# A relational graph network: weights by matmul, fewer paced gathers, another order at each layer's end

## Chip, core and metric

The kernel runs on one core of a Trainium2 chip. The metric is the device time of one execution in microseconds, taken as the median of the runs shown. A trace of one further execution, taken by the hardware profiler, gives the durations.

The engines are named as in the profile. PE multiplies matrices, DVE is the vector engine, ACT copies and scales, POOL issues the gathers, and SP issues most other transfers.

## What is computed

There are 12500 nodes with 128 features and 200000 edges in 8 relations, sorted by their target node. Two layers run one after the other, and then a residual and a normalization of each row.

```python
W = jnp.einsum('rb,bio->rio', comp, basis)
xw = jnp.einsum('ni,rio->nro', x, W)
msgs = xw[src, et]
seg = dst * N_REL + et
summed = jax.ops.segment_sum(msgs, seg, num_segments=N_NODES * N_REL)
cnt = jax.ops.segment_sum(jnp.ones((msgs.shape[0],), x.dtype), seg, num_segments=N_NODES * N_REL)
mean = summed / jnp.maximum(cnt, 1.0)[:, None]
agg = mean.reshape(N_NODES, N_REL, HIDDEN).sum(axis=1)
return agg + x @ root + bias
# for each layer: h = relu(conv(h)) + h ; at the end: layernorm(x + h)
```

## The kernel before

**Tiles.** The edges are cut into 1563 tiles of 128. Eight tiles make an octet; there are 196, numbered 0 to 195, and the last has three tiles. Each tile is one indirect gather of 128 rows of 512 bytes, issued by POOL (L632). Layer 0 gathers rows of the input x. Layer 1 gathers rows of y_d, a table in DRAM that holds h times each of the eight relation weights, for every node.

**Order.** The program writes its instructions into a `Plan`. `Plan.add` takes the cells that an operation reads and writes, and works out the semaphore waits; each engine runs its own instructions in the order in which they were added. Transfers use semaphore lanes in turn, three of them for gathers ("gq"), and an operation on a lane waits for the one before it on that lane.

**Gathers and pacing.** `gather(l, q)` issues octet q of layer l. The loops call it with `o + AHEAD`, five octets ahead of the octet that PE takes, and there are seven buffers of rows. `slower` says after which gathers POOL also clears a small tile named rest (L641): 256 columns for the first 160 gathers of layer 0, 320 columns for the last 48 of each layer. Before each such memset POOL waits for the one before the previous one.

**Relation weights.** w_sb holds the nine weight matrices of each layer (eight relations and the root). `weight(l, r)` makes one of them on DVE: one multiplication and seven fused multiply-adds over the eight bases (L656 and L661). Layer 0's are made before the loop, behind the masks of octets 0 and 1. Layer 1's are in the list `later`, which the loop takes from when the counting of edges (`prep`) has ended.

**Layer 0.** For octet o, DVE makes one-hot masks dm with the mean's weights in them (`onehot`, L940). PE multiplies the gathered rows by them (`means`, L1015) into two PSUM banks s, and ACT copies these to sT (`take_means`). `product` multiplies sT by the eight weights (L1038) and `take_product` copies the result to ys. `place` puts it with a mask pl (L948) at its nodes (L1069), and adds the root's term (L1071). When a block of 128 nodes has all its edges, `close` makes the two steps of `finish`: DVE adds the carried part and the bias (L1087, L1092), and then forms h (L1111). `end` runs the second step and calls `table` for the block: two halves on PE (L1127), each copied to y_row, and stored to y_d. Blocks run from 0 to 97; the last two are stored by halves, one of which DVE copies (L1134). `batch` runs the copies that are due, and `table_now` does one half at once. The order of the last octets is written out by hand after the loop.

**Layer 1.** Its first gather waits for the whole of y_d. `add_rows` multiplies each octet by masks of 256 columns straight into an accumulator of a block (L1169), with the root's term (L1172). `finish` follows, and for every eight blocks `norm`: transposes on PE (L1194), and statistics, scaling and the store of the output (L1203 to L1222). Two calls of `onehot` lead the loop, and masks have two buffers here.

Of the kernel before, what the change touches and what calls it, by code (L numbers as in the profile page):

```python
# [8 lines left out]
F32 = mybir.dt.float32  # L9
# [290 lines left out]
class Plan:  # L300
# [25 lines left out]
    def add(self, eng, emit, reads=(), writes=(), lane=None, n=1):  # L326
# [9 lines left out]
        for c in reads:  # L336
            if c in self.writer:
                need(raw, self.writer[c])
# [83 lines left out]
def ordered_path(  # L422
# [46 lines left out]
    AHEAD = 5  # L469
    H = R // 2  # L470
# [16 lines left out]
    y_d = dram.tile([N * R, D], F32, name="y_d")  # L487

# [40 lines left out]
    b_sb = b_f(arena).rearrange("p (l b d) -> p l b d", l=L, b=NB)  # L529
# [5 lines left out]
    def h_cells(j):  # L535
# [9 lines left out]
        ("p_r", I32), ("p_rf", F32))}  # L545
# [33 lines left out]
    plan = Plan(tc, {"hw": 8, "aq": 4, "gq": 3})  # L579
# [33 lines left out]
    rest = keep([P, PACE, 320], F32, "rest")  # L613
# [3 lines left out]
    def slower(l, i):  # L617
        if l == 0 and i < 160:
            return 256
        return 320 if i >= T - 48 else 0  # L620

    def gather(l, q):
# [6 lines left out]
        def emit():  # L629
            ins = []  # L630
            for i in range(q * Q, min((q + 1) * Q, T)):
                ins.append(nc.gpsimd.indirect_dma_start(  # L632
                    out=t[:, i - q * Q, :], out_offset=None, in_=x if l == 0 else y_d,
                    in_offset=bass.IndirectOffsetOnAxis(ap=ids[:, i:i + 1], axis=0)))
                n = slower(l, i)
                if n:
                    k = slow[0]
                    slow[0] += 1
                    if k >= PACE:
                        nc.gpsimd.wait_ge(paced, k - PACE + 1)  # L640
                    nc.gpsimd.memset(rest[:, k % PACE, :n], 0).then_inc(paced, 1)  # L641
            return ins

# [43 lines left out]
    def start():  # L687
# [24 lines left out]
        load(b_sb[:, 0], basis[0].rearrange("b i o -> i b o"), [], [("b_sb", 0)])  # L712
# [6 lines left out]
        load(b_sb[:, 1], basis[1].rearrange("b i o -> i b o"), [], [("b_sb", 1)])  # L719
# [95 lines left out]
    def where():  # L815
# [192 lines left out]
    def means(o):  # L1008
# [4 lines left out]
        def emit():  # L1013
            for i in range(n):
                last = nc.tensor.matmul(s_b[i // 4][0][:, i % 4, :], t[:, i, :], d[:, i, :], start=True, stop=True)  # L1015
            return last

        pe(emit, [c] + dc, [s_b[h][1] for h in range(-(-n // 4))])
# [137 lines left out]
    def add_rows(q, k, opens, last):  # L1156
# [5 lines left out]
        reads = [c] + dc  # L1162
        if root_in:
            ht, hc = hT[:, k * P:k * P + rows_of(k)], ("h", k)
            reads += [hc, ("w", 1, R)]

        def emit():
            for i in range(n):
# [317 lines left out]
```

## Time and profile before

| what | value |
|---|---|
| median of 3 runs | 4023.44 us (4021.93 to 4025.25) |
| profiled execution, its own time | 4022.45 us |
| its span in the trace | 4020.1 us |
| POOL busy | 3055.4 us (76%), 3390 instructions |
| PE busy / weight loads | 2535.3 us (63%) / 2052.8 us (51%) |
| DVE busy | 1701.9 us (42%) |
| ACT busy | 387.7 us (10%) |
| gathers of layer 0 / layer 1 | 1563 x 953 ns / 1563 x 944 ns |
| first gather of layer 1 starts at | 2037.83 us |

A busy share is a mean over the span and does not say what the end waits for. "Issue" is time in which an engine waited for nothing that the profile shows. In a group of the profile the numbers after the bar are the busy time in us and the mean of one instruction in ns, and then the idle time before them with what ended it. A line of the timeline or of the chain starts with its start and its duration in us. A wait line has its total, its count and its longest. A matmul of 32-bit floats shows as two records in the trace, so an octet of eight tiles shows as x16.

### The profile page before, as it was taken

The page shows a single profiled execution, that of the slowest core. Times are in us where ns is not written, and L with a number is a line of the kernel's source. Part 1 is how long each engine was busy: PE and PEld are TensorE (multiplying, and loading weights), DVE is VectorE, ACT ScalarE, POOL GpSimd, SP SyncE. Part 2 cuts the span into 40 slices and gives each one's busy share as a digit, 9 for nine tenths or more (in the row PEclk, how much of TensorE's full clock was granted, in tenths as well). Part 3 has the DMA queues.
Part 4 walks back from the last instruction along what each step waited for, and adds up shares of the span by engine and source line. Part 5 has one row for each costly group of instructions (what it writes and reads, how often), then busy time and mean ns, then how long its engine had stood idle before and what let it go on. Part 6 is the DMA issues. An engine that isn't in the chain of part 4 may idle for free.

```text
span 4020.1 us, 32388 instructions
## 1 busy us (share of the span) xinstructions
PE 2535.3 (63%) x11205; PEld 2052.8 (51%) x11205; DVE 1701.9 (42%) x4764; ACT 387.7 (10%) x834; POOL 3055.4 (76%) x3390
## 2 busy tenths in 40 slices
PE   5776677776666666667655565566556555555654
PEld 3555565555555555556544444444444444444443
DVE  7667533333333333333234444444444444444443
ACT  1111122221111111112100000000000000000000
POOL 8887777777777777777857777777777777777777
PEclk8988888888888888888877777777777777777777
DMA  3112233332222222223222222222222222222221
GB/s 106 50 48 53 58 105 100 105 96 83 80 89 81 83 85 79 85 75 95 73 74 53 58 58 63 53 63 64 53 64 63 53 63 53 63 63 53 63 59 45
DMA packets 128800, 282.48 MB, mean 70 GB/s; under 512 B 53855, under 2 KB 61291, under 8 KB 128627
## 3 DMA queue, kind: packets, MB, share of 16 engines
q0 software_dynamic: 100032, 205.07, 19.6%
q1 hardware_dynamic: 25546, 73.59, 5.0%
q10 hardware_dynamic: 3049, 1.67, 0.2%
q8 instruction: 90, 1.47, 0.2%
q14 instruction: 83, 0.68, 0.1%
HBM read 222.52 MB, written 57.60 MB: 70 GB/s over the span
## 4 chain that ended last, share of the span: by engine, by line
POOL 73%; issue 23%; PE 2%; DVE 1%; DMA 1%; ACT 0%; POOLq 0%; DVEq 0%; ACTq 0%; SPq 0%
POOL rows L632 71%; POOL rest L641 2%; DVE w_sb L661 1%; PE s L1015 0%; PE y L1038 0%; PE ct L772 0%; DMA rows<-in_x_dram,idx 0%; DVE dm L940 0%; PE ct L773 0%; PE s L1169 0%; PE pt L1127 0%; POOLq L397 0%; DVE arena L766 0%; DMA arena<-in_dst_dram 0%; PE ct L1038 0%
## 5 line engine op out<-in xcount | busy, mean ns | idle before, releaser
L632 POOL DMA_INDIRECT rows<-y_d,idy x1563 | 1476.0, 944 | 495.6 <-issue 469.5
L632 POOL DMA_INDIRECT rows<-in_x_dram,idx x1563 | 1489.0, 953 | 449.5 <-issue 446.0
L940 DVE TENSOR_SCALAR dm<-cols,near,w 128x256 f32<-128x256 f32 x1563 | 724.0, 535 | 1099.5 <-PE s L1169 732.3
L1169 PE MATMUL s<-dm,rows 128*128 128x256 f32 x2086 | 744.1, 527 | 517.9 <-DMA rows<-y_d,idy 498.9
L1169 PEld LDWEIGHTS s<-dm,rows 128*128 128x128 f32 x2086 | 555.7, 277 | 674.0 <-DVE dm L940 272.4
L1015 PE MATMUL s<-dm,rows 128*128 128x128 f32 x3126 | 572.0, 358 | 510.3 <-DMA rows<-in_x_dram,idx 510.2
L1015 PEld LDWEIGHTS s<-dm,rows 128*128 128x128 f32 x3126 | 528.0, 263 | 636.4 <-DMA rows<-in_x_dram,idx 577.6
L940 DVE TENSOR_SCALAR dm<-cols,kr,w 128x128 f32<-128x128 f32 x1563 | 514.6, 400 | 603.5 <-PE s L1015 491.3
L1169 PE MATMUL ct<-dm,rows 128*128 128x256 f32 x1040 | 365.7, 521 | 263.7 <-DMA rows<-y_d,idy 252.2
L1169 PEld LDWEIGHTS ct<-dm,rows 128*128 128x128 f32 x1040 | 273.8, 274 | 340.0 <-DVE dm L940 153.7
L1038 PE MATMUL y<-w_sb,sT 128*128 128x128 f32 x1824 | 276.0, 316 | 31.9 <-ACT sT L599 31.9
L1038 PEld LDWEIGHTS y<-w_sb,sT 128*128 128x128 f32 x1824 | 268.5, 233 | 37.6 <-ACT sT L599 37.6
L599 ACT ACTIVATE sT<-s 128x512 f32<-128x512 f32 x391 | 213.5, 607 | 223.5 <-PE s L1015 223.5
L1087 DVE TENSOR_TENSOR v<-po,carry 128x128 f32<-128x128 f32 x98 | 28.4, 290 | 479.3 <-PE s L1015 322.9
L1127 PE MATMUL pt<-w_sb,arena 128*128 128x512 f32 x388 | 204.4, 608 | 36.7 <-ACT y_row L599 35.0
L599 ACT ACTIVATE y_row<-pt 128x512 f32<-128x512 f32 x194 | 115.8, 597 | 1152.8 <-PE s L1015 1051.6
L1215 ACT ACTIVATE st<-st,eps 128x8 f32<-128x8 f32 (+1 forms) x13 | 4.0, 308 | 1968.8 <-DVE dm L940 1839.4
L1038 PE MATMUL ct<-w_sb,sT 128*128 128x128 f32 (+1 forms) x1312 | 187.3, 304 | 0.0
L1038 PEld LDWEIGHTS ct<-w_sb,sT 128*128 128x128 f32 (+1 forms) x1312 | 184.1, 223 | 0.8 <-issue 0.8
L1069 PE MATMUL po<-pl,ys 128*128 128x256 f32 x392 | 117.9, 383 | 0.0
L1127 PEld LDWEIGHTS pt<-w_sb,arena 128*128 128x128 f32 x388 | 63.5, 190 | 83.0 <-ACT y_row L599 77.3
L948 DVE TENSOR_SCALAR pl<-cols,pos 128x256 f32<-128x256 f32 x196 | 92.6, 472 | 26.8 <-PE s L1015 17.6
(125 smaller groups left out, 1092.8 us busy)
## 6 DMA issues: line engine op xcount, KB each, us to landing
y_d<-y_row SPq DMA_DIRECT2D x96, 512.0 KB, 2.8
rows<-in_x_dram,idx POOLq DMA_INDIRECT x1563, 2.5
rows<-y_d,idy POOLq DMA_INDIRECT x1563, 2.5
x_g<-in_x_dram SPq DMA_DIRECT2D x24, 512.0 KB
out_dram<-x_g SPq DMA_DIRECT2D x12, 512.0 KB, 3.2
arena<-in_L_gnn_basis_dram SPq DMA_DIRECT2D x2, 512.0 KB
arena<-in_dst_dram ACTq DMA_DIRECT2D x2, 448.0 KB, 11.9
arena<-in_edge_type_dram SPq DMA_DIRECT2D x2, 448.0 KB
```

The costliest lines, as they stand in the source:

```text
L599: act(lambda: nc.scalar.activation(out_t, in_t, AF.Copy), reads, writes)
L632: ins.append(nc.gpsimd.indirect_dma_start(out=t[:, i - q * Q, :], out_offset=None, in_=x if l == 0 else y_d, in_offset=bass.IndirectOffset ...
L641: nc.gpsimd.memset(rest[:, k % PACE, :n], 0).then_inc(paced, 1)
L661: vec(lambda b=b: nc.vector.scalar_tensor_tensor(w_sb[:, l, r, :], b_sb[:, l, b, :], comp_sb[:, c0 + b:c0 + b + 1], w_sb[:, l, r, :], op0= ...
L940: emits.append(lambda i=i: nc.vector.tensor_scalar(t[:, i - q * Q, :wide], cols[:, :wide], ids[:, i:i + 1], w[:, i:i + 1], op0=ALU.is_equa ...
L948: emits.append(lambda: nc.vector.tensor_scalar(o[:m], cols[:m], pos[:m, g // (2 * R), g % (2 * R):g % (2 * R) + 1], None, op0=ALU.is_equal))
L1015: last = nc.tensor.matmul(s_b[i // 4][0][:, i % 4, :], t[:, i, :], d[:, i, :], start=True, stop=True)
L1038: last = nc.tensor.matmul(y[:m], t[:, r, :nt, :].rearrange("p t k -> p (t k)"), w_sb[:, 0, r, :], start=(r == 0), stop=(r == R - 1))
L1069: ins = nc.tensor.matmul(a, o[:m], t[:m], start=opens, stop=last and not root_in)
L1087: emits.append(lambda: nc.vector.tensor_add(v[:, :n], a[:, :n], t[:, :n]))
L1127: pe(lambda: nc.tensor.matmul(hb[:n].rearrange("p r d -> p (r d)"), hT[:, j * P:j * P + n], w_sb[:, 1, k * H:(k + 1) * H, :].rearrange("p ...
L1169: ins = nc.tensor.matmul(a, t[:, i, :], d[:, i, :], start=(opens and i == 0), stop=(last and i == n - 1))
```

## The change

It does three things. `weights` makes all eight relation matrices of a layer by two matmuls: the bases are loaded as (basis, group of rows) by (row in group, column), a matrix `mixer` holds the coefficients of both layers spread over those groups, ACT copies the products to a y_row buffer, and two transfers on SP write them to w_d in DRAM and read them back into w_sb in the layout needed. `slower` now paces the first 96 gathers of layer 0 and no others. And the last six octets of each layer are gathered two octets ahead of PE instead of five, behind a wait (`after`) for the octet that PE has last been given; the last but one octet is gathered and multiplied in two halves. The order of the last octets of layer 0 is written out anew, and its loop ends two octets earlier. There are four gather lanes.

```diff
-    def add(self, eng, emit, reads=(), writes=(), lane=None, n=1):
+    def add(self, eng, emit, reads=(), writes=(), lane=None, n=1, after=()):
...
-        for c in reads:
+        for c in (*reads, *after):
...
+    CLOSE = 2
+    LATE = 6
...
+    w_d = dram.tile([L, R * D, D], F32, name="w_d")
...
-    b_sb = b_f(arena).rearrange("p (l b d) -> p l b d", l=L, b=NB)
+    b_sb = b_f(arena).rearrange("p (l c) -> p l c", l=L)
...
+    pick = keep([P, NB + K], F32, "pick")
+    mix = keep([P, L * R], F32, "mix")
+    mixer = keep([P, L * R, K], F32, "mixer")
...
-    plan = Plan(tc, {"hw": 8, "aq": 4, "gq": 3})
+    plan = Plan(tc, {"hw": 8, "aq": 4, "gq": 4})
...
-    rest = keep([P, PACE, 320], F32, "rest")
+    rest = keep([P, PACE, 256], F32, "rest")
...
     def slower(l, i):
-        if l == 0 and i < 160:
-            return 256
-        return 320 if i >= T - 48 else 0
+        return 256 if l == 0 and i < 96 else 0
...
-        plan.add("POOL", emit, reads, [cell], lane="gq", n=min(Q, T - q * Q))
-
-    def weight(l, r):
-        c0 = (l * R + r) * NB
-
-        def emit0():
-            return nc.vector.tensor_scalar(w_sb[:, l, r, :], b_sb[:, l, 0, :], comp_sb[:, c0:c0 + 1], None,
-                                           op0=ALU.mult)
-
-        vec(emit0, [("b_sb", l), "comp"], [("w", l, r)])
-        for b in range(1, NB):
-            vec(lambda b=b: nc.vector.scalar_tensor_tensor(
-                w_sb[:, l, r, :], b_sb[:, l, b, :], comp_sb[:, c0 + b:c0 + b + 1], w_sb[:, l, r, :],
-                op0=ALU.mult, op1=ALU.add), [], [("w", l, r)])
+
+        def some(i0, i1):
+            def emit():
+                ins = []
+                for i in range(i0, i1):
+                    ins.append(nc.gpsimd.indirect_dma_start(
+                        out=t[:, i - q * Q, :], out_offset=None, in_=x if l == 0 else y_d,
+                        in_offset=bass.IndirectOffsetOnAxis(ap=ids[:, i:i + 1], axis=0)))
...
+        i0, n = q * Q, in_quad(q)
+        after = [("done", l)] if q >= NQ - LATE else []
+        if q == NQ - 2:
+            for h in range(2):
+                plan.add("POOL", some(i0 + h * 4, i0 + h * 4 + 4), reads, [cell + (h,)], lane="gq", n=4, after=after)
+        else:
+            plan.add("POOL", some(i0, i0 + n), reads, [cell + (0,), cell + (1,)], lane="gq", n=n, after=after)
+
+    def gathers(l, o):
+
+        if o + AHEAD < NQ - LATE:
+            gather(l, o + AHEAD)
+        elif NQ - LATE <= o + CLOSE < NQ:
+            gather(l, o + CLOSE)
+        return o + CLOSE == NQ - 1
+
+
+    def mixers():
+        for op, val, a, f in ((ALU.logical_shift_right, 4, "p_b", "p_bf"), (ALU.bitwise_and, K - 1, "p_r", "p_rf")):
+            vec(lambda op=op, val=val, a=a: nc.vector.tensor_single_scalar(small[a], part, val, op=op), ["part"], [a])
+            vec(lambda a=a, f=f: nc.vector.tensor_copy(small[f], small[a]), [a], [f])
+        vec(lambda: nc.vector.tensor_scalar(pick[:, :NB], iota_f[:, :NB], small["p_bf"], None, op0=ALU.is_equal),
+            ["iota", "p_bf"], ["pick0"])
+        vec(lambda: nc.vector.tensor_scalar(pick[:, NB:NB + K], iota_f[:, :K], small["p_rf"], None, op0=ALU.is_equal),
+            ["iota", "p_rf"], ["pick1"])
+        c3 = comp_sb.rearrange("p (m b) -> p m b", b=NB)
+        vec(lambda: nc.vector.tensor_tensor(c3, c3, pick[:, None, :NB].to_broadcast([P, L * R, NB]), op=ALU.mult),
+            ["pick0"], ["comp"])
+        vec(lambda: nc.vector.tensor_reduce(mix, c3, axis=AX.X, op=ALU.add), ["comp"], ["mix"])
+        vec(lambda: nc.vector.tensor_tensor(mixer, mix.unsqueeze(2).to_broadcast([P, L * R, K]),
+                                            pick[:, None, NB:NB + K].to_broadcast([P, L * R, K]), op=ALU.mult),
+            ["mix", "pick1"], ["mixer"])
+
+    def weights(l, banks):
+        o, oc = yr_r.tiles[l], ("y_row", l)
+        of = o.rearrange("p r d -> p (r d)")
+        for h in range(2):
+            b, bc = banks[h]
+            pe(lambda b=b, h=h: nc.tensor.matmul(b.rearrange("p t d -> p (t d)"),
+                                                 mixer[:, l * R:(l + 1) * R, :].rearrange("p r k -> p (r k)"),
+                                                 b_sb[:, l, h * 4 * P:(h + 1) * 4 * P], start=True, stop=True),
+               ["mixer", ("b_sb", l)], [bc])
+            copy(of[:, h * 4 * P:(h + 1) * 4 * P], b.rearrange("p t d -> p (t d)"), [bc], [oc + (h,)])
+        load(w_d[l].rearrange("(p i) o -> p (i o)", i=R), of, [oc + (0,), oc + (1,)], [("w_d", l)])
+        load(w_sb[:, l, :R, :], w_d[l].rearrange("(r i) o -> i r o", r=R), [("w_d", l)], [("w", l, r) for r in range(R)])
...
-        load(b_sb[:, 0], basis[0].rearrange("b i o -> i b o"), [], [("b_sb", 0)])
+        load(b_sb[:, 0], basis[0].rearrange("b (h i) o -> (b h) (i o)", i=R), [], [("b_sb", 0)])
...
-        load(b_sb[:, 1], basis[1].rearrange("b i o -> i b o"), [], [("b_sb", 1)])
+        load(b_sb[:, 1], basis[1].rearrange("b (h i) o -> (b h) (i o)", i=R), [], [("b_sb", 1)])
...
-        for op, val, a, f in ((ALU.bitwise_and, G - 1, "p_in", "p_inf"), (ALU.logical_shift_right, 3, "p_g", "p_gf"),
-                              (ALU.bitwise_and, K - 1, "p_r", "p_rf")):
+        for op, val, a, f in ((ALU.bitwise_and, G - 1, "p_in", "p_inf"), (ALU.logical_shift_right, 3, "p_g", "p_gf")):
...
-        pe(emit, [c] + dc, [s_b[h][1] for h in range(-(-n // 4))])
+        def some(i0, i1):
...
+        if o == NQ - 2:
+            for h in range(2):
+                pe(some(4 * h, 4 * h + 4), [c + (h,)] + dc, [s_b[h][1], ("done", 0)])
+        else:
+            pe(some(0, n), [c + (0,), c + (1,)] + dc, [s_b[h][1] for h in range(-(-n // 4))] + [("done", 0)])
...
+        if q == NQ - 2:
+            for h in range(2):
+                pe(some(4 * h, 4 * h + 4), [c + (h,)] + dc + more, [ac, ("done", 1)])
+        else:
+            pe(some(0, n), [c + (0,), c + (1,)] + dc + more, [ac, ("done", 1)])
...
-    for q in range(2):
-        onehot(0, q)
-    for r in range(R):
-        weight(0, r)
+    onehot(0, 0)
+    mixers()
+    weights(0, po_b)
+    onehot(0, 1)
...
-    later = [lambda r=r: weight(1, r) for r in range(R)] + [lambda b=b: check_edges(b) for b in range(B)]
+    later = [lambda: weights(1, (pt_b, pt_b))] + [lambda b=b: check_edges(b) for b in range(B)]
...
-    for o in range(NG - 1):
-        gather(0, o + AHEAD)
+    for o in range(NG - 3):
+        gathers(0, o)
...
-    for i in (g - 2, g - 1):
-        onehot(0, NQ, i)
+    def placed(o):
+        close(place(o))
+        for step in opened:
+            step()
+        opened.clear()
+        end()
+
+    gathers(0, g - 2)
+    for step in opened:
+        step()
+    opened.clear()
     batch(None)
     end()
-    close(place(g - 3))
+    product(g - 3)
+    onehot(0, g, g - 4)
+    placed(g - 5)
+    take_product(g - 3)
+    placed(g - 4)
+    onehot(0, NQ, g - 3)
+    placed(g - 3)
+    while len(tables) > 2:
+        table_now()
+    means(g - 2)
+    take_means(g - 2)
+    onehot(0, NQ, g - 2)
+    product(g - 2)
+    take_product(g - 2)
+    while tables:
+        table_now()
+    placed(g - 2)
+    onehot(0, NQ, g - 1)
     onehot(0, NQ, g)
+    means(g - 1)
+    take_means(g - 1)
+    means(g)
+    take_means(g)
     product(g - 1)
     take_product(g - 1)
-    opened.pop()()
-    end()
-    place(g - 2)
-    while tables:
-        table_now()
-    means(g)
-    take_means(g)
-    close(place(g - 1))
-    opened.pop()()
-    end()
-    table_now()
     product(g)
     take_product(g)
-    table_now()
-    close(place(g))
-    opened.pop()()
-    end()
-    while tables:
-        table_now()
+    placed(g - 1)
+    placed(g)
+    now = tables[:]
+    tables.clear()
+    for h in (0, 2):
+        for a, _ in now[h:h + 2]:
+            a()
+        for _, b in now[h:h + 2]:
+            b()
...
-        gather(1, q + AHEAD)
-        if q + AHEAD == NQ - 1:
+        if gathers(1, q):
             pool(lambda: nc.gpsimd.drain())
```

More of the change, by code (lines that the diff above doesn't have):

```diff
@@ L544, in ordered_path @@
         ("nb_i", I32), ("nb_n", F32), ("p_in", I32), ("p_inf", F32), ("p_g", I32), ("p_gf", F32),
-        ("p_r", I32), ("p_rf", F32))}
+        ("p_r", I32), ("p_rf", F32), ("p_b", I32), ("p_bf", F32))}
+    pick = keep([P, NB + K], F32, "pick")
+    mix = keep([P, L * R], F32, "mix")
+    mixer = keep([P, L * R, K], F32, "mixer")
     sel = keep([P, G, K], F32, "sel")
@@ L627, in gather @@
         ids = idx if l == 0 else idy
[L629 to L642, printed above, removed]
         b = q * Q // P
@@ L649, in gather @@
             reads += [("y_d", j) for j in range(NT - 2)] + [("y_d", j, k) for j in (NT - 2, NT - 1) for k in (0, 1)]
-        plan.add("POOL", emit, reads, [cell], lane="gq", n=min(Q, T - q * Q))
-    def weight(l, r):
-        c0 = (l * R + r) * NB
-        def emit0():
-            return nc.vector.tensor_scalar(w_sb[:, l, r, :], b_sb[:, l, 0, :], comp_sb[:, c0:c0 + 1], None,
-                                           op0=ALU.mult)
-        vec(emit0, [("b_sb", l), "comp"], [("w", l, r)])
-        for b in range(1, NB):
-            vec(lambda b=b: nc.vector.scalar_tensor_tensor(
-                w_sb[:, l, r, :], b_sb[:, l, b, :], comp_sb[:, c0 + b:c0 + b + 1], w_sb[:, l, r, :],
-                op0=ALU.mult, op1=ALU.add), [], [("w", l, r)])
+        def some(i0, i1):
[5 more added lines that the diff above has]
+                        in_offset=bass.IndirectOffsetOnAxis(ap=ids[:, i:i + 1], axis=0)))
+                    n = slower(l, i)
+                    if n:
+                        k = slow[0]
+                        slow[0] += 1
+                        if k >= PACE:
+                            nc.gpsimd.wait_ge(paced, k - PACE + 1)
+                        nc.gpsimd.memset(rest[:, k % PACE, :n], 0).then_inc(paced, 1)
+                return ins
+            return emit
@@ L1011, in means, with emit @@
         n = in_quad(o)
[L1013 to L1016, printed above, removed]
-        pe(emit, [c] + dc, [s_b[h][1] for h in range(-(-n // 4))])
+        def some(i0, i1):
+            def emit():
+                for i in range(i0, i1):
+                    last = nc.tensor.matmul(s_b[i // 4][0][:, i % 4, :], t[:, i, :], d[:, i, :], start=True, stop=True)
+                return last
+            return emit
+        if o == NQ - 2:
[3 more added lines that the diff above has]
+            pe(some(0, n), [c + (0,), c + (1,)] + dc, [s_b[h][1] for h in range(-(-n // 4))] + [("done", 0)])
         plan.mark("PE")
@@ L1161, in add_rows, with some, emit @@
         root_in = opens and k >= 0
-        reads = [c] + dc
+        more = []
         if root_in:
             ht, hc = hT[:, k * P:k * P + rows_of(k)], ("h", k)
-            reads += [hc, ("w", 1, R)]
-        def emit():
-            for i in range(n):
-                ins = nc.tensor.matmul(a, t[:, i, :], d[:, i, :], start=(opens and i == 0),
-                                       stop=(last and i == n - 1))
-                if i == 0 and root_in:
-                    nc.tensor.matmul(a[:, :rows_of(k)], w_sb[:, 1, R, :], ht, start=False, stop=False)
-            return ins
-        pe(emit, reads, [ac])
+            more += [hc, ("w", 1, R)]
+        def some(i0, i1):
+            def emit():
+                for i in range(i0, i1):
+                    ins = nc.tensor.matmul(a, t[:, i, :], d[:, i, :], start=(opens and i == 0),
+                                           stop=(last and i == n - 1))
+                    if i == 0 and root_in:
+                        nc.tensor.matmul(a[:, :rows_of(k)], w_sb[:, 1, R, :], ht, start=False, stop=False)
+                return ins
+            return emit
+        if q == NQ - 2:
[3 more added lines that the diff above has]
+            pe(some(0, n), [c + (0,), c + (1,)] + dc + more, [ac, ("done", 1)])
         plan.mark("PE")
@@ L1352, in ordered_path @@
     g = NG - 1
-    assert parts is None and not later and not turned_to and not opened
+    assert parts is None and not later and not turned_to
     def table_now():
```

## Prediction

> **What bounds the kernel now.** I read the page's chain first, then its groups with shapes kept apart, then the waits, then the chain and timeline around the layer's turn.
>
> ```profile
> POOL 73%; issue 23%; PE 2%; DVE 1%; DMA 1%; ACT 0%; POOLq 0%; DVEq 0%; ACTq 0%; SPq 0%
> ...
> POOL rows L632 <- issue: 915.4, 3120, 0.3
> POOL rows L632 <- DMA y_d<-y_row: 26.1, 1, 26.1
> ...
> L641 POOL MEMSET rest<- 128x256 f32 x160 | 53.4, 334 | 0.1
> ...
> L641 POOL MEMSET rest<- 128x320 f32 x96 | 36.6, 381 | 0.1
> ```
>
> 96% of the chain is POOL and its issue time. Of the 4020 us, 3126 gathers use 1489.0 + 1476.0 us and the 915.4 us of issue time between them. POOL waits for other engines once, 26.1 us for layer 0's table; PE makes it wait 1.1 us in all. So what POOL no longer does is time, and what leaves DVE, PE or ACT is not, unless POOL waits for it.
>
> The next lines (POOL in the timeline) give the pitch with and without pacing.
>
> ```profile
> 1938.88 0.94 POOL L632 DMA_INDIRECT rows<-in_x_dram,idx  x1 [0.30 <-issue]
> 1940.13 0.94 POOL L632 DMA_INDIRECT rows<-in_x_dram,idx  x1 [0.30 <-issue]
> 1941.08 0.38 POOL L641 MEMSET rest<- 128x320 f32 x1
> 1941.62 0.95 POOL L632 DMA_INDIRECT rows<-in_x_dram,idx  x1 [0.17 <-issue]
> 1942.57 0.38 POOL L641 MEMSET rest<- 128x320 f32 x1
> 1943.12 0.95 POOL L632 DMA_INDIRECT rows<-in_x_dram,idx  x1 [0.17 <-issue]
> ```
>
> An unpaced gather comes every 1.248 us, one with a 320 memset every 1.495. In the chain near 106 us, gathers with a 256 memset start at 106.58 and 108.02: 1.442. Each memset thus costs 0.247 or 0.194 us of POOL, less than its own 0.38 or 0.33, since part of it lies in issue time.
>
> The last view is PE in the timeline, late in layer 0 (the last line is from the chain).
>
> ```profile
> 1907.74 2.05 PE L1015 MATMUL s<-dm,rows 128*128 128x128 f32 x16
> 1917.72 3.78 PE L1015 MATMUL s<-dm,rows 128*128 128x128 f32 x16 [3.04 <-DMA rows<-in_x_dram,idx]
> 1927.67 2.05 PE L1015 MATMUL s<-dm,rows 128*128 128x128 f32 x16 [1.69 <-DMA rows<-in_x_dram,idx]
> ...
> 1984.69 3.28 PE L1015 MATMUL s<-dm,rows 128*128 128x128 f32 x16 [2.30 <-DMA rows<-in_x_dram,idx]
> ...
> 2008.53 3.23 PE L1015 MATMUL s<-dm,rows 128*128 128x128 f32 x16 [2.26 <-DMA rows<-in_x_dram,idx]
> ...
> 2034.77 2.29 DMA y_d<-y_row
> ```
>
> Unpaced octets come every 10.0 us, and PE waits for each one's landing, about 1.6 us after its last gather is issued. Even at full rate PE keeps up with POOL. Octet 194 starts on PE at 2008.53, octet 195's last gather is issued by 2011.3 (it lands near 2012.9), and layer 1's first gather starts at 2037.83, behind the y_d store.
>
> **The change, part by part.**
>
> *Start pacing.* Memsets go from gathers 96 to 159: 64 x 0.194 = **12.4 us**, all on POOL. Is there cover for the faster pace? Octets 21 to 34 are already unpaced while the counts of later blocks run, and their gathers start every 10.1 to 10.4 us; PE waited for them. So octets 12 to 19 should run like that.
>
> A rule bears on this. Row first: in the chain one gather at 142.78 took 2.47 us, not 0.95; the long ones of the first 400 us lie mostly over the f16 comparisons of L766, and the stretch above 0.945 adds up to about 12.8 us in layer 0. The Trainium skill (SBUF — State Buffer, Who interferes with whom) says that a VectorE instruction with two SBUF inputs contends with a GpSimd one that reads SBUF. Taken alone, it prices the removed w_sb operations, two SBUF inputs each, at up to their 39.4 us as gain, and lets the unpaced gathers meet more L766. The trace disagrees on the first: gathers during the w_sb stage (29 to 52 us) keep the 11.5 us octet, and w_sb overlaps account for about 0.4 us of stretch. I take 0 for w_sb, and for L766 the same stretch as now, because the number of those operations is unchanged: bounds -3 to +4 us.
>
> *Weights.* Removed: 64 DVE operations per layer, in the first layer from 28.92 to 52.41, 23.5 us; in the second the same beside gathers. Added on DVE: four 128x1 operations (0.15 each by L822/L823), two masks (0.31 by L826), a product and a reduction over 128 columns (0.29 each by L859/L860), a 128x256 product (0.5, by the 0.44 of L828): 2.3 us. Two of the small ones come out of the later placement code. Per layer also two 128x512 matmuls (1.1 each by L1127), two ACT copies (0.6 each), a 512 KB store to DRAM (2.8, by the y_d row) and its read back in 512-byte pieces. No row shows that read; it lies between the 2.3 of y_d and, with other work, 7.8 of the root load; I take 3.5. With dm of octet 0 done at 26.4, layer 0's weights arrive about 26.4 + 2.3 + 2.2 + 0.7 + 2.8 + 3.5 = 38, up to 43, instead of 52.4. They are first needed by product(0), and POOL does not need PE's first octet until gather 56, at 88 us. So this gives POOL **0**; if the cover were gone the bounce would cost 6 to 11 us once. Queues: on SP the two DMAs stand behind x_g (its issue ends near 27.7) and SP waits there for ACT; behind it are only later loads of x. ACT's queue is passed by two copies. In layer 1 the weights go between octets 27 and 42, with SP idle, and the first table is at 42. One instruction order matters: PE's means(0) now stands behind the weight matmuls, at about 31 instead of 27.2; nothing waits for it before 88 us.
>
> *Lead.* The last six gathers of a layer also wait for PE's octet three back. PE ends that octet about 6 us after its landing, some 12 us before POOL wants to issue (octet 187 on PE ends near 1929.7; gather 190 would start near 1946). So **0**. Behind a blocked gather on POOL stand all later gathers and, in layer 1, only the drain. The fourth lane and the half-and-half octet 194 add one wait each: 0.
>
> *End of layer 0.* Gathers 1515 up to octet 192's landing lose 28 memsets, 6.9 us: PE starts 192 at 1984.7 - 6.9 = 1977.8 on this run's clock, before the start's gain. From there I follow PE's new order, with octet 192 at 0 and the landings of 193, 194, 195 at 10, 20 and 23.7. Means 192 (3.5), product 191 (2.4) and a placement: 6.4. Product 192 (1.95), placements 190 to 192 with their DVE steps: 11.1. Four table halves of blocks 93 and 94 at 1.81 (2019.07 to 2020.88 in the chain), PE free at 17.6. Means 193 (2.05) 19.7, its ACT copies 1.1, product 193: 22.8. The halves of 95: 25.6, placement 193: 26.6. Means 194 and 195 (2.05 + 0.83): 29.4. Products 194 and 195 (3.9): 33.3. Placements 194, 195 (1.7): 35.0. Four last halves, copied on ACT and DVE by turns: last copy out at 40.0. Store 2.3, POOL's start 0.75: 43.0. So layer 1 starts at 1977.8 + 43.0 = 2020.8, not 2037.8: **17.0 us**. PE, no longer POOL, sets this stretch: everything has landed by 23.7.
>
> Here the second rule matters. The rows: sixteen matmuls take 2.05 us after continuous work and 3.78 after a 3 us wait. The skill (TensorE: Matmul & The Clock Gate, What's actually happening) says that an idle window drops the array to half clock and that some 3.4 us of work restore it. In the new order PE is rarely idle after octet 192, so I take warm durations. Were it cold throughout, three means add 1.7 and four products 1.1 each, about 8 to 10 us, and the gain is 8. If instead the order were limited by octet 195's landing alone, the last steps (means, products, placements, halves, store) take about 15 us after it, and the gain is 21.6. Range 8 to 21.6.
>
> *End of layer 1.* Octet 193 lands 36 x 0.247 = 8.9 us earlier. Now PE's octet 193 (6.8), dm (1.5), wide (0.3), and the normalization of eight slots on PE and DVE run to about 16.2 after its landing, and the last v follows at 17.1; before it was at 4005.19 - 3986.39 = 18.8. Gain 8.9 + 1.7 = **10.6**. Bounds 9 (half-octet gives nothing) to 12.5 (all 48 memsets and shorter). The final store and exit are unchanged.
>
> Sum: 12.4 + 0 + 17.0 + 10.6 = 40.0 us. The profiled execution took 4022.45 (span 4020.1), so 3982.4; the median of the runs shown is 1.0 higher: **3983 us**.
>
> **The rivals.**
> *Late PE at the turn* (20%). PE runs cold or is already late at octet 192; only 8 of the 17 remain: 3992. For: octets 191 to 192 hold 9.7 us of PE work (1996.62 to 2006.27 shows one like it), close to the 10.0 pitch. Against: two rows in three at that pitch are warm.
> *Ideal turn* (14%): PE has caught up, and less stretch by L766 adds 3: 40 + 4.6 + 3 gives 3975.
> *Pacing protected the gathers* (6%): without memsets the gathers of octets 12 to 19 stretch as much as the memsets took; the start gives 0: 3995. Against: octets 21 to 27.
> *Lead becomes a serial wait* (4%), slower: if PE ends the octet three back later than POOL finishes the two between, over 14 us behind its landing, each of 12 late octets waits for PE. At 4.5 us each this is 54 us, against the 40 gained: 4037. It decides only from 3.4 us per octet. The trace shows PE under 7 us behind.
> That the weights arrive late is no rival with this size: it would need 45 us more.
>
> **How the numbers follow.** The main case has 56%, range 3978 to 3988. With late PE, ideal turn and the stretch beside it, the range is 3972 to 3995; outside lie the ends of these and the lead. 0.2% is 8 us, about what a measurement of this kernel can tell from no change. All but the lead, and 2% of odd sums, are faster by more: 0.94; same 0.02; slower 0.04.
>
> **What would show it.** Memsets: 96 of 128x256, none of 320. Gathers 96 to 159 every 1.25 to 1.29 us; the last 48 of each layer every 1.25. L656 and L661 of w_sb gone, PE's octet 2 near 50 and not 72 us, yet POOL's octets 0 to 11 where they were. POOL's wait on y_d near 21 us, from 26.1. POOL waits on PE below 2 us. It is wrong if POOL waits for s or for a PE semaphore in the late octets, if gathers 96 to 159 keep 1.4 us, or if that wait on y_d grows.

## The result, and the profile after

The changed kernel takes 3979.64 us (median of 5 runs, 3978.35 to 3979.88). Beside it the kernel before took 4023.44 us (5 runs, 4021.93 to 4025.65). The ratio is 0.989, with a 95% interval of 0.9875 to 0.9904. The prediction was 3983 us in a range of 3972 to 3995, so time and direction were right. The profiled execution took 3979.88 us, with a span of 3978.1.

First the page's chain, which answers to the one shown of before:

```profile
POOL 74%; issue 23%; PE 2%; DMA 1%; DVE 0%; POOLq 0%; ACT 0%; ACTq 0%; SPq 0%
```

Then POOL's groups with shapes kept apart:

```profile
L645 POOL DMA_INDIRECT rows<-in_x_dram,idx x1563 | 1488.2, 952 | 465.0 <-issue 460.0 <-DMA arena<-in_dst_dram 2.5 <-PE y L1084 0.6
L645 POOL DMA_INDIRECT rows<-y_d,idy x1563 | 1476.6, 945 | 495.1 <-issue 495.1
L654 POOL MEMSET rest<- 128x256 f32 x96 | 31.9, 332 | 0.1
```

And its longest wait line, with the total, the count and the longest single wait:

```profile
POOL rows L645 <- issue: 955.1, 3117, 19.2
```

POOL still bounds the kernel, with 97% of the chain. The gathers take what they took (952 and 945 ns, before 953 and 944). Of the 256 memsets 96 are left. The issue time is 955.1 instead of 915.4 us. Of the 39.7 more, 20.5 are pauses that a removed memset no longer covers (160 of them, each 0.30 instead of 0.17 us, make 20.8). The other 19.2, the longest, is the wait at the turn of the layers, which this trace puts under "issue" and not under y_d.

The chain at that turn shows what it really is:

```profile
2001.69 0.70 DVE y_row L1180
2002.39 0.02 issue
2002.40 2.54 DMA y_d<-y_row
...
2005.07 1.00 issue
2006.07 0.94 POOL rows L645
```

The last half of the table is copied, stored in 2.54 us, and POOL starts layer 1 at 2006.07, before at 2037.83.

To place the gain I cut the span at three gathers of POOL. The second pair of profiles comes from the experiments, where both kernels ran once more on a chip on which the kernel before takes 4023 us.

| stretch of POOL | before, two profiles | after, two profiles | gain | predicted |
|---|---|---|---|---|
| start to layer 0's octet 188 | 1926.4, 1926.8 | 1913.5, 1914.7 | 12.9, 12.1 | 12.4 |
| octet 188 to layer 1's first gather | 111.4, 112.5 | 92.6, 92.6 | 18.8, 19.9 | 17.0 |
| that gather to layer 1's octet 188 | 1878.2, 1878.3 | 1879.1, 1879.9 | -0.9, -1.6 | 0 |
| octet 188 to the end of the span | 104.1, 105.2 | 92.9, 94.1 | 11.2, 11.1 | 10.6 |
| sum | 4020.1, 4022.8 | 3978.1, 3981.3 | 42.0, 41.5 | 40.0 |

### The profile page after: what moved, and what is told of

Read it like the earlier page. It is cut to its first block, busy times and chain, and to the rows that moved or that the text cites. A ratio compares the mean times of both kernels' runs of the same rounds, so it can differ in the third digit from the quotient of the medians.

```text
span 3978.1 us, 32124 instructions
## 1 busy us (share of the span) xinstructions
PE 2532.4 (64%) x11213; PEld 2046.9 (51%) x11213; DVE 1660.6 (42%) x4643; ACT 390.6 (10%) x838; POOL 2997.6 (75%) x3230
## 4 chain that ended last, share of the span: by engine, by line
POOL 74%; issue 23%; PE 2%; DMA 1%; DVE 0%; POOLq 0%; ACT 0%; ACTq 0%; SPq 0%
POOL rows L645 73%; POOL rest L654 1%; PE s L1055 0%; DMA rows<-in_x_dram,idx 0%; PE y L1084 0%; PE pt L1173 0%; PE ct L1084 0%; POOLq L398 0%; PE s L1216 0%; PE po L1115 0%; DVE x_g L1275 0%; DMA y_d<-y_row 0%; DMA rows<-y_d,idy 0%; DMA idx<-in_src_dram 0%; ACT y_row L606 0%
```

## The experiments

The twelve runs fell on three chips of the same kind. On chip A the kernel before takes 4023 us, on chip B about 4655 and on chip C 4611, so each run is compared with the kernel before on its own chip. The first expectations, those of chip B, were written with chip A's times in mind; the later ones give numbers for both sorts of chip.

### On chip A: the change again, its lead, its table halves

The changed kernel once more:

> The changed kernel itself, on the chip of the experiments. Where PE keeps up with the gathers (the kernel before takes about 4023 us) it should take 3980 us, ratio 0.989. Where PE lags the landings by some 70 us (the kernel before takes about 4653 us) the serial-wait reading says that octet 190's first gather waits 30 to 35 us behind PE in layer 0 and about 10 to 15 us in layer 1, so that it ends near the other kernels with the lead of two, 4716 to 4740 us, above the kernel before. The rival says the loss of those kernels came from their own edits (more pacing, less pacing, DVE weights), and then this one takes at most what the kernel before takes there, about 4610 to 4655 us.

Measured: 3980.23 us (3978.01 to 3983.2), before 4023.43, ratio 0.9891 (0.9875 to 0.9908). The result repeats. The kernel before, for a second profile:

> The kernel before, for a profile on the chip of the experiments. Where PE lags by some 70 us: PE is the bound of both layers' bodies, so octets 20 to 188 are as far behind the gathers as in the kernel with only the pacing changed; the stage from PE's octet 189 to layer 1's first gather takes about 58 to 65 us, against 86 to 90 with the lead of two. If the kernel with only the pacing changed lost its 0.7% by PE's clock, the bodies of the layers and not the stages at their ends will be shorter here.

Measured: 4025.05 us in one execution; its stretches are in the table above. This chip was of the first sort, so the comparison of PE-bound bodies that it was meant for did not come about.

Next, the lead of five for all octets and no wait for the octet last given to PE:

```diff
-        after = [("done", l)] if q >= NQ - LATE else []
+        after = []
...
-        if o + AHEAD < NQ - LATE:
-            gather(l, o + AHEAD)
-        elif NQ - LATE <= o + CLOSE < NQ:
-            gather(l, o + CLOSE)
-        return o + CLOSE == NQ - 1
+        gather(l, o + AHEAD)
+        return o + AHEAD == NQ - 1
```

> The changed kernel with the lead of five throughout and without the wait for the octet that PE has last been given; everything else as changed. Where PE keeps up: the wait has never ended last, so no difference to the changed kernel (within 3 us, about 3980 us). Where PE lags by some 70 us: octet 190's gather no longer waits in either layer, PE's octet 189 to layer 1's first gather takes about 58 us instead of 86 to 90, and PE's octet 189 of layer 1 to its end about 49 instead of 59, so some 40 us less than the changed kernel. If the lead is not what costs there, both take the same within the noise of 25 us, and the two stages are the same.

Measured: 3977.26 us (3975.86 to 3978.12), ratio to before 0.9885 (0.9869 to 0.9902). That is 3.0 us under the changed kernel on the same chip, at the edge of the 3 us that were called no difference. POOL's stretches are 1913.8, 90.7, 1878.4 and 92.6: the late gathers keep their pitch, so the wait costs POOL nothing. Of the 1.9 us at the turn, 1.6 are PE's, in octet 192. PE in the timeline, first of this kernel, then of the changed one:

```profile
1965.02 2.05 PE L1052 MATMUL s<-dm,rows 128*128 128x128 f32 x16 [0.56 <-DMA rows<-in_x_dram,idx]
1966.91 1.95 PE L1081 MATMUL ct<-w_sb,sT 128*128 128x128 f32 x16
```

```profile
1964.74 3.64 PE L1055 MATMUL s<-dm,rows 128*128 128x128 f32 x16 [3.03 <-DMA rows<-in_x_dram,idx]
1968.21 1.95 PE L1084 MATMUL ct<-w_sb,sT 128*128 128x128 f32 x16
```

The same sixteen matmuls take 2.05 us behind a table half with 0.56 us idle, and 3.64 after 3.03 us idle. From their start to the product it is 1.89 against 3.47. The second profile of the changed kernel has this for octets 191 and 192:

```profile
1955.99 3.54 PE L1055 MATMUL s<-dm,rows 128*128 128x128 f32 x16 [1.46 <-DMA rows<-in_x_dram,idx]
...
1965.97 3.67 PE L1055 MATMUL s<-dm,rows 128*128 128x128 f32 x16 [1.54 <-DMA rows<-in_x_dram,idx]
```

So octets were slow after 1.46 and 1.54 us idle, while a line shown of before was warm (2.05) after 1.69; the idle time alone does not say which it will be. The trace does say why a half stood next to octet 192 with the lead of five: octet 191 was slow there (3.78 us), its products were slow too (2.86), and the half behind them ended only 0.56 us before octet 192 landed. But octet 191 was fast (2.00) in one profile of the changed kernel and slow (3.54) in the other, so this changes from execution to execution. The 1.6 us cannot be put down to the lead.

Last, table halves on two PSUM banks for five blocks instead of two:

```diff
         split = j >= NT - 2
+        other = j >= NT - 5
...
-            hb, bc = ct_b if split and k == 1 else pt_b
+            hb, bc = ct_b if other and k == 1 else pt_b
```

> The changed kernel with the two halves of the table alternating between two PSUM banks for the last five blocks of layer 0 instead of the last two. The turn of the layers is bound by PE; where a half on one bank waits for the copy of the half before it, a half is issued after about 1.8 us instead of 1.1. Expected: PE's octet 192 to layer 1's first gather 2 to 4 us shorter than in the changed kernel, and nothing elsewhere: a ratio of 0.999 to the changed kernel, which the times alone hardly show. A rival says that the copies on ACT set the pace whichever bank they come from, and the stage is as long as before.

Measured: 3977.82 us (3977.45 to 3981.07), ratio to before 0.9887 (0.987 to 0.9903), which does not part it from the changed kernel. The stage is 1.6 us shorter (octet 192 on PE to layer 1's first gather 39.7 against 41.3 in both profiles of the changed kernel; octet 192 is slow in all three), just below the expected 2 to 4. PE in the timeline of this kernel says where the rest went:

```profile
1976.74 1.02 PE L1174 MATMUL pt<-w_sb,arena 128*128 128x512 f32 x2
...
1979.41 1.02 PE L1174 MATMUL ct<-w_sb,arena 128*128 128x512 f32 x2
1980.27 1.95 PE L1055 MATMUL s<-dm,rows 128*128 128x128 f32 x16
...
1987.65 1.95 PE L1055 MATMUL s<-dm,rows 128*128 128x128 f32 x16
1991.94 0.91 PE L1055 MATMUL s<-dm,rows 128*128 128x128 f32 x6 [2.34 <-DMA rows<-in_x_dram,idx]
```

The four halves of blocks 93 and 94 take 3.5 us instead of 6.3 (1975.00 to 1981.30 in the changed kernel), and the two of block 95, behind octet 193, take 1.7 instead of 2.7. So the rival, that ACT's copies set the pace, is out. But of these 3.7 us PE gives back most: it now reaches octet 195 before its rows have landed and waits 2.34 us for them, where the changed kernel did not wait. There PE's work and the landing of octet 195 are nearly in balance at the turn, and a shorter PE order alone has little more to give.

### On chips B and C: where PE does not keep up

Five kernels ran on chip B and three on chip C. They were to split the gain by part. That failed, since POOL is not the bound there. The measured times stand together in a table behind the expectations.

More start pacing, 160 gathers, in the changed kernel:

```diff
-        return 256 if l == 0 and i < 96 else 0
+        return 256 if l == 0 and i < 160 else 0
```

> The changed kernel with the memset after each of the first 160 gathers of layer 0 again, instead of 96. Theory (each memset is POOL time and PE keeps up either way): 64 x 0.194 = 12.4 us more by the pitches, up to 13.4 by the start of octet 20 in the two traces; 3992 to 3993 against 3979.6, all of it between octets 12 and 20. Rival (the start gained because the weights left DVE, and the memsets are hidden): 3980 and octet 20 near 231.

Pacing at both layers' ends, in the changed kernel:

```diff
-        return 256 if l == 0 and i < 96 else 0
+        if l == 0 and i < 96:
+            return 256
+        return 320 if i >= T - 48 else 0
```

> The changed kernel with the 320-column memset after each of the last 48 gathers of both layers again. Theory: octet 192 of layer 0 lands 6.9 us later and the PE work behind it follows unchanged, with about 2 more because octet 195 now lands after PE wants it; in layer 1 10.6 to 12 more. Together 19 to 21 us: 3999 to 4001. Rival (the end of layer 0 is bound by PE's order alone, so that late landings are free there): 10.6 to 12 us only, 3990 to 3992. Rival (the memsets spared the matmuls or the landings something): under 3985.

No pacing, in the changed kernel:

```diff
-        return 256 if l == 0 and i < 96 else 0
+        return 0
```

> The changed kernel with no memset at all. Theory: 96 x 0.194 = 18.6 us off POOL; PE's first octet ends near 37 us and octet 7 would be gathered from about 75, so no wait: 3961. Rival (gathers are stretched by the f16 comparisons of the counting as the pace rises, or PE, which takes 8.5 to 9 us an octet there, makes POOL wait): half of it, 3970. Rival (the first memsets protect the input transfers, and without them everything starts later): 3980 or more.

Only the new pacing, in the kernel before (on chip B, then once more on C):

```diff
-        if l == 0 and i < 160:
-            return 256
-        return 320 if i >= T - 48 else 0
+        return 256 if l == 0 and i < 96 else 0
```

> The kernel before with one edit: memsets after the first 96 gathers of layer 0 and nowhere else; DVE weights, lead of five, old order. Theory: start 12.4 to 13.4; layer 0's end only by the landing of octet 194, 10.9, because PE's old order takes 29.3 us from there; layer 1's end 9 to 12. Together 32 to 36 us: 3987 to 3991. The rest, 8 to 11 us, would be the new order's. Rival (pacing is everything): 3980. Rival (the old order falls behind at the faster pitch, PE late): 3996 or more.

> The kernel before with only the pacing of the changed kernel (96 gathers of layer 0), lead, order and weights as before. Where PE keeps up (before about 4023 us): the start gains 12.4 us, the octets at each layer's end come every 10 us instead of 12, so octet 194 of each layer lands about 10.7 us earlier. In before the turn takes 29.3 us from octet 194's means to layer 1's first gather; if that stays, layer 1 starts 23 us earlier and the end gains another 9 to 10.5, in all 33 to 35 us, 3988 to 3991 us, ratio 0.9915 to 0.992. The rest of the changed kernel's gain, 8 to 10 us, is then the new order and the halves. If the order of before makes PE late already from octet 192 on, the turn gains less, the total is 25 to 30 us, 3993 to 3998 us. Where PE lags by some 70 us it takes about 0.7% longer than the kernel before again.

Weights on DVE, in the changed kernel (on B, then on C):

```diff
-    onehot(0, 0)
-    mixers()
-    weights(0, po_b)
-    onehot(0, 1)
+    for q in range(2):
+        onehot(0, q)
+    for r in range(R):
+        weight(0, r)
...
-    later = [lambda: weights(1, (pt_b, pt_b))] + [lambda b=b: check_edges(b) for b in range(B)]
+    later = [lambda r=r: weight(1, r) for r in range(R)] + [lambda b=b: check_edges(b) for b in range(B)]
```

> The changed kernel with the relation weights made on DVE again (64 operations a layer, bases loaded as before, no mixer, no matmuls, no transfers through w_d); pacing, lead and order as changed. Theory (POOL sets the time and does not wait for PE at the start): no difference, within 2 us of the changed kernel, where that takes 3979.6; octet 20 of layer 0 is gathered from 231 to 233 and PE's octet 2 runs near 72 instead of 54. Rival (the start gained because PE is ready earlier): PE's first octets 20 us later make POOL wait in octets 7 to 14, up to 20 us slower. Rival (the weights through DRAM cost time): faster by 2 to 10 us. If PE is the slower engine in this run, the first rival's 20 us should show in full.

> The changed kernel with the weights made by 128 two-operand instructions on DVE as before; pacing, lead and order as changed. Where PE keeps up: the matmul weights are hidden, so no difference to the changed kernel, 3978 to 3982 us, ratio 0.989; octet 0's product waits for the weights until about 55 us and the catch-up on PE is over before octet 20. The rival (reads of weights and bases by DVE stretch the gathers of POOL) expects 5 to 10 us more, lying between octets 2 and 30.

No pacing, lead of five and halves on two banks, three of the edits above together:

```diff
-        return 256 if l == 0 and i < 96 else 0
+        return 0
...
-        after = [("done", l)] if q >= NQ - LATE else []
+        after = []
...
+        gather(l, o + AHEAD)
+        return o + AHEAD == NQ - 1
...
+        other = j >= NT - 5
```

> The changed kernel with three more edits: no pacing at all, the lead of five throughout, and the table halves alternating banks for the last five blocks of layer 0. Where PE keeps up: without the 96 memsets the start gains 96 x 0.194 = 18.6 us more (octet 20 starts at about 213 instead of 232), the turn 1.5 to 3 us, nothing at the end: 3956 to 3960 us, ratio 0.983 to 0.985. The rival that the remaining pacing protects the first gathers from colliding with something (loads of the start, PE not yet through with the buffers) expects that the start gives back half of it or more: octet 20 at 222 or later, 3965 to 3980 us.

| kernel, chip | median us | before there | ratio, 95% |
|---|---|---|---|
| more start pacing, B | 4740.06 (two near 4704, two near 4772) | 4653.04 | 1.0187 (1.0086 to 1.0288) |
| pacing at the ends, B | 4720.91 | 4653.04 | 1.0102 (1.0011 to 1.0194) |
| no pacing, B | 4736.76 | 4653.04 | 1.0163 (1.0089 to 1.0236) |
| only the new pacing, B | 4689.61 | 4653.04 | 1.0069 (1.0031 to 1.0108) |
| weights on DVE, B | 4715.76 | 4657.34 | 1.0147 (1.006 to 1.0234) |
| only the new pacing, C | 4658.1 | 4610.76 | 1.009 (1.0067 to 1.0113) |
| weights on DVE, C | 4657.6 | 4610.76 | 1.0092 (1.0066 to 1.0119) |
| three edits, C | 4681.36 | 4610.76 | 1.0136 (1.0088 to 1.0184) |

All are slower than the kernel before there, though the kernels of chip B lie too close together for their spread of up to 72 us to be ranked. The expectation for only the new pacing on C, written after chip B's result, gave about 0.7% more time for this case; it is 0.9%. The times that the other expectations give are for a PE that keeps up, and none was reached here. The profile of the kernel with only the new pacing, on chip C, shows what the bound is there. Span and mean granted clock of its core:

```profile
core 0: 4653.1 us, clock 0.732
```

The page's busy row and chain:

```profile
PE 2431.6 (52%) x11205; PEld 1924.6 (41%) x11205; DVE 1696.3 (36%) x4764; ACT 387.2 (8%) x834; POOL 3004.7 (65%) x3230
...
another core or an unknown queue 44%; PE 22%; DVE 18%; issue 11%; ACT 4%; DMA 0%; POOL 0%; DVEq 0%; POOLq 0%; ACTq 0%; SPq 0%
```

POOL's waits:

```profile
POOL rows L630 <- remote: 480.0, 137, 9.9
POOL rows L630 <- PE s L1013: 166.2, 27, 9.4
```

POOL's share of the chain is 0%. It waits some 650 us in these two lines together; the second is for buffers that PE has not freed, and that the 480 us of the first ("remote", a release that the profile does not show) are the same is likely but not shown. PE's mean granted clock is 0.73 there, 0.80 to 0.81 on chip A. PE's matmuls do not fill the time either: it is busy 52% of the span and stops for up to tens of microseconds in between. It does not stop alone. Of the kernel with more start pacing, PE, ACT and DVE in the timeline:

```profile
261.29 1.95 PE L1055 MATMUL s<-dm,rows 128*128 128x128 f32 x16
316.12 3.42 PE L1084 MATMUL y<-w_sb,sT 128*128 128x128 f32 x16 [52.87 <-issue]
```

```profile
314.98 1.08 ACT L606 ACTIVATE sT<-s 128x512 f32<-128x512 f32 x2 [54.56 <-remote]
```

```profile
314.98 0.29 DVE L1133 TENSOR_TENSOR v<-po,carry 128x128 f32<-128x128 f32 x1 [56.14 <-remote]
```

PE, ACT and DVE stand for over 50 us and start again within 1.2 us of each other, while POOL issues 42 gathers. The six profiles of the kernels on chip A, with the two of the result, have no stretch of over 8 us in which none of the three works. The eight of chips B and C have 74 to 86 each, 927 to 1234 us in sum. POOL issues gathers in every one of these 627 stops, and in none is there a memset: they lie where the gathers are not paced.

The kernels without any pacing stop from the start. DVE and then POOL in the timeline of no pacing, on chip B:

```profile
54.58 0.72 DVE L806 TENSOR_TENSOR arena<-arena 128x153 f16<-128x153 f16 x4 [21.01 <-issue]
77.01 0.70 DVE L806 TENSOR_TENSOR arena<-arena 128x157 f16<-128x157 f16 x4 [21.71 <-remote]
```

```profile
103.61 0.94 POOL L645 DMA_INDIRECT rows<-in_x_dram,idx  x1 [29.17 <-PE s L1055]
```

From 22 us on the counting of edges stands for 11, 20 and 21 us with little work between. PE begins its first octet at 101.1 us (34.4 in the changed kernel on chip A), and POOL waits 29 us for it at octet 7. Octet 12 is gathered at 163.5 us and not at 148.0 as with more start pacing, from which this kernel differs by its memsets alone; with three edits on chip C it is 161.3, with weights on DVE 148.4. So the memsets that were to cost 18.6 us saved 13 to 16 us there. The rival of the last expectation, that pacing protects the first gathers, said octet 20 at 222 us or later; it is at 264.4 on B and 262.3 on C. Pacing at the ends points the same way, though that kernel as a whole is not faster: octet 180 on PE to layer 1's first gather takes 159.5 us with it, and 172.8 to 178.4 in the other changed kernels of chip B. By what a stream of unpaced gathers stops the other engines, and why not on chip A, no run shows. Nor is it shown whether the lower clock there is a cause or a consequence of a PE that stands so often.

After such a stop PE stays 63 to 69 us behind the gathers. So more start pacing and DVE weights (160 and 96 paced gathers) are equal again at octet 100 on chip B: PE starts it at 1330 and 1336 us, though octet 20 was at 261 and 322.

These chips do test one rival of the prediction, the lead as a serial wait, because there PE is over 14 us behind. Weights on DVE (lead two) and only the new pacing (lead five), both on chip C, POOL in the timeline at octet 190 of layer 0:

```profile
2305.25 0.94 POOL L645 DMA_INDIRECT rows<-in_x_dram,idx  x1 [34.60 <-PE s L1040]
```

```profile
2284.86 0.95 POOL L630 DMA_INDIRECT rows<-in_x_dram,idx  x1 [8.28 <-PE s L1013]
```

The wait is there, 34.6 us, and 21.0 again in layer 1, where the lead of five waits 0.3. From such waits on chip B I had worked out that the lead costs some 40 us where PE lags; that is the number in the expectation of the lead of five. Longer stretches say otherwise. From PE's octet 180 to layer 1's first gather, lead two takes 170.0 us on chip C against 168.1 and 166.6 with five; on chip B 172.8, 176.1 and 178.4 (more start pacing, DVE weights, no pacing) against 166.6. From PE's octet 180 of layer 1 to the end of octet 195 it is the other way round: 131.8 against 139.1 and 133.9 on C, and 130.8, 124.1 and 130.1 against 141.5 on B. So the kernels with lead two are 2 to 12 us longer at the turn and shorter again at the end: PE, which POOL waits for there, still has rows in its buffers while POOL stands. These kernels differ in more than the lead, so this is no clean measurement of it; only the new pacing also has the old order at the turn. The pair most alike in the ends, both with the new order, is weights on DVE and three edits on chip C: 3.4 us longer at the turn, 2.1 shorter at the end. A cost of 40 us does not fit any of these stretches.

Why all eight are slower than the kernel before on B and C stays open. All have fewer memsets than it, and less pacing alone costs 0.7% and 0.9%. But more pacing at one place in the changed kernel, at the start or at the ends, did not mend it, and there is no profile of the kernel before on those chips. The changed kernel itself did not run on B or C.

## Why the prediction was right

**Start pacing.** Predicted 12.4 us, measured 12.9 and 12.1 up to octet 188. Octets 12 to 19 now come every 10.1 to 10.4 us (in the second profile 10.1 to 10.6, once 11.0). That they stretch as octets 21 to 34 did is seen here: POOL in the timeline of the changed kernel.

```profile
152.18 0.94 POOL L645 DMA_INDIRECT rows<-in_x_dram,idx  x1 [0.31 <-issue]
153.43 1.13 POOL L645 DMA_INDIRECT rows<-in_x_dram,idx  x1 [0.30 <-issue]
```

A gather here and there is 0.2 us longer, not every one. What layer 0's gathers took above 0.945 us each adds up to 13.1 and 14.4 us in the two profiles, before to 14.3 and 15.4 (the prediction had about 12.8 for before). So the rival in which pacing protected the gathers of octets 12 to 19 is out on this chip. For a start without any pacing, and on the other chips, it is not: see above. The gain of up to 39.4 us that the Trainium skill (SBUF — State Buffer, Who interferes with whom) could have given to the removed weight operations did not come: layer 0 up to octet 188 gained 12 to 13 us, which the memsets account for.

**Weights.** Predicted 0 for POOL. Octet 12, the first after the paced ones, starts at 149.7 and 148.6 us, before at 150.1 and 149.9: nothing, within 1.3 us. The kernel with weights on DVE never ran on chip A; on chip B, with the same start pacing, its octet 12 starts at 148.2 us and that of the kernel with matmul weights (pacing at the ends) at 147.3. Octet 0's product starts on PE at 42.04 us, inside the 38 to 43 given:

```profile
30.77 3.78 PE L697 MATMUL po<-arena,mixer 128*128 128x512 f32 x4 [0.92 <-DVE mixer L688]
34.35 2.81 PE L1055 MATMUL s<-dm,rows 128*128 128x128 f32 x16
...
42.04 2.05 PE L1084 MATMUL y<-w_sb,sT 128*128 128x128 f32 x16
```

The two weight matmuls took 3.78 us, not the 2.2 that I took from a row of a busy PE; octet 0's means began at 34.35 and not 31. Both are hidden, as said: POOL needs nothing of PE before 88 us. PE's octet 2 comes at 53.7 and 52.8 us, before at 71.9 and 73.1, and POOL gains nothing from it.

**Lead.** Predicted 0, and POOL waits for PE 2.4 us in all, against "below 2". The lead of five took 3.0 us less; 1.6 us of that is a warmer octet on PE, which changes between executions, and none is a wait of POOL. That PE would be close behind the gathers is a thing of this chip: where it is 63 us behind, the wait of the rival is there.

**End of layer 0.** Predicted 17.0, measured 18.8 and 19.9. The first term was right: octet 188's gather to octet 192 on PE fell by 7.1 us (58.3 to 51.2; 6.9 predicted). The path after it was 43.0 and measured 41.3. PE's order holds its times with warm durations: octet 193 at 16.6 (17.6), the last copy out at 37.7 (40.0), then 3.7 to POOL's start (3.05). Octet 193 had landed near 10, so PE set this stretch, as said. PE's path was thus 2.3 us too long in the prediction, in small pieces (1.0 up to octet 193, 0.7 from there to octet 194, 0.6 to the last copy), and the store with POOL's start 0.6 too short. Behind octet 192 no means ran slow: sixteen matmuls took 1.95 us in octet 193, and the 22 of octets 194 and 195 took 2.68. So the 8 to 10 us for a cold array were not paid. Neither late PE nor the ideal turn came true: the gain lies between 17.0 and 21.6, and PE waited for no landing behind octet 192.

**Between.** Layer 1's body lost 0.9 and 1.6 us where 0 was predicted. The pauses are the same; the gathers themselves took 1.0 to 1.7 us more in sum (1420.9 and 1421.7 against 1419.8 and 1420.0). Why is not known; with the lead of five the stretch is 1878.4, as before.

**End of layer 1.** Predicted 10.6, measured 11.2 and 11.1. Octet 193 reaches PE 9.0 us earlier (8.9), and the last v follows 15.9 us behind it (17.1 predicted, 18.8 before), so 2.9 and not 1.7 came from there; behind the last v 0.7 was lost again. The end of octet 193, octet 194 and octet 195 on PE:

```profile
3954.52 1.16 PE L1247 MATMUL po<-ident,wide 128*128 128x128 f32 x8 [1.74 <-DVE wide L1157]
3955.51 3.62 PE L1216 MATMUL s<-dm,rows 128*128 128x256 f32 x16
3960.55 0.70 PE L1216 MATMUL s<-dm,rows 128*128 128x256 f32 x2 [1.42 <-DMA rows<-y_d,idy]
```

PE goes from the transposes straight into octet 194 and waits 1.42 us for octet 195. The last gather of octet 194 ends on POOL at 3954.85; if its rows land the 1.6 us later that the prediction read from before, PE would have had to wait until about 3956.5 for the whole octet, so the halves are worth about 1 us here (an estimate). The octet itself takes 3.62 us; before, it and one tile of the next took 5.84.

The sum of the profiles is 42.0 and 41.5 against 40.0. Of the 3.4 us between 3983 and 3979.64 the stretches hold 2.0, nearly all of it from the end of layer 0; the rest is the spread of executions (the medians differ by 43.8, the profiled executions by 42.6). How much of the ends is less pacing and how much is the new order was not separated on chip A: the traces give 7.1 and 9.0 us up to where PE takes over, and 11.7 and 2.2 behind it, where octets 193 to 195 still come faster too.

One thing was luck: the prediction says nothing of the chip. The time was measured where POOL is the bound, as in the trace that the prediction was read from. On chips B and C no kernel with parts of this change was faster than the kernel before.

## What to carry to other kernels

When one engine holds nearly all of the chain, the cost of an edit to it is a count times a difference of starts (0.194 and 0.247 us for a memset that lasts 0.33 and 0.38), read where the edit is and where it is not. Where another engine takes over for a stretch, as PE does at the turn, follow that engine's order step by step from the last landing, and look at once for what it would wait for next: six shorter table halves saved 3.7 us and 2.3 of them became a wait for octet 195. Before a pause is taken out of one engine, look at what the others do where the pause is missing already, and on more than one chip: 18.6 us of memsets left out made octet 12 come 13 to 16 us later on two of them. A long wait of an engine that is not the bound, 34.6 us here, is no measure of what it costs; compare a longer stretch of the whole.

## What was not expected of the hardware

Chips of one kind differ: the kernel before takes 4023, 4611 and 4655 us on three of them. On the slower two the granted clock is 0.73 to 0.74 instead of 0.80 to 0.81, and PE, ACT and DVE stop together for tens of microseconds at a time (52.87 us of PE in the line above) while POOL issues gathers without a memset between them. The kernel before with less pacing, which only takes work from POOL, is 0.7% and 0.9% slower. A gain worked out where POOL is the bound holds only for chips where it is.
